# A third third-level Strassen product in half products of u (token groups 2 and 3), with three operand sums made by accumulating DMAs

## Chip, cores and metric

The kernel runs on one core of one Trainium2 chip. The metric is the device time of one execution in microseconds; the kernel before takes 812.7 us (median of three runs, 812.04 to 813.1). All data are float32.

## What is computed

The reference takes x of shape (4, 1024, 1024), four sequences of 1024 tokens. It normalises each token, and then

```python
g    = sigmoid(einsum('btd,ed->bte', u, gate_w) + gate_b)    # u is the normalised x
u_g  = u * g                                                 # its mean over a sequence enters d_eff
...                                                          # a recurrence over u_g gives s
h    = silu(xr @ w1.T)                                       # xr: the 4096 normalised tokens
h    = silu(h @ w3.T)
h    = h @ w2.T
for k in range(TOP_K):                                       # two of eight experts for each token
    out = out.at[indices_k[:, k]].add(gates[:, k:k + 1] * h) # only rows 0 to 7 are ever written
x    = x + s * silu(out)
```

Only the first eight rows of `out` differ from zero, so only those need the recurrence. What costs time is three products with 1024 x 1024 weights: `gate_w` (called g), `w1` (called u) and `w3` (called m).

## The kernel before

The 4096 tokens are taken in four groups of 1024 (`sb` = 0 to 3). Group 0 computes g, u and m, groups 1 to 3 compute u and then m, so that the order of the stages is u and g of group 0, m0, u1, m1, u2, m2, u3, m3. (Rows 0 to 7 lie in the first sequence, which is group 0, so g is needed for group 0 alone.)

Each stage is a 1024 x 1024 x 1024 product. It is done as Strassen's algorithm (Winograd's form) on two levels: seven half products `i`, in the order 1, 2, 5, 6, 7, 4, 3 for u (`order`), each of 512 x 512 x 512, and in each of these seven products of 256 x 256 x 256, the *steps* 0 to 6 of `Half.step`. One such product is four matmuls of 128 x 128 weights against 256 columns (`small`). A `block` is an operand of 128 x 4 x 512 values, a `quarter` one of 128 x 512. The left operand of half product 1, 2 and 4 is a block of tokens; that of 5, 6, 3 and 7 is a sum s1, s2, s4, s3 of blocks (`S_OF`): s1 = a21 + a22, s2 = s1 - a11, s4 = a12 - s2, s3 = a11 - a21. From its operand `left_sums` makes four quarters for the second level. All of this is subtraction on POOL (four instructions of 128x512 for a block in groups 1 to 3). The sums of the weights are made in group 0 or 1, kept in HBM (`kept`) and loaded again in the later groups.

In groups 1 to 3 some of the 256-cubed products are themselves split by Strassen: seven matmuls of 128 columns in place of four of 256. Such a product is called a *leaf*. `leaves_of` gives their number in a half product: two in u of groups 2 and 3 and in m of group 3, one elsewhere. Each leaf needs four sums of its token operand (`token_thirds`: three POOL instructions, one of 128x256 and two of 128x128) and four of its weights (`weight_thirds`: four instructions of 128x128, once, in group 1 for u; then `load_thirds`). `Half.third` issues its matmuls in phases: "a", "b", "c" write into the PSUM tile W and add from it into the result `dst` on DVE; "2" puts the rest of the first leaf into Y, "3" the rest of the second into Z, and phase "0" is the addition of the first product from the PSUM tile X.

Two half products are interleaved. Each has a place on a time line in units of one product (some 1.7 us), seven units apart; `at(place, f)` queues work, `run_todo` emits it, and all instructions stay in the program order thus made on each engine. With S the start of a half product, its steps 0 to 6 stand at S + 0, 2, 4.5, 5.5, 8, 6, 10.5, its phases "0", "a", "b", "c" at S + 1.9, 5.2, 7.5, 8.8. Within one period of seven units PE therefore runs:

1. step 0 of the current half product (into X),
2. phase "b" of the previous one,
3. its step 4 (into the previous X),
4. its phase "c",
5. step 1 of the current one (Z),
6. step 6 of the previous one (its X, the last),
7. step 2 of the current one (X again, accumulating on what step 0 left),
8. phase "a", steps 3 (Y) and 5 (Z) of the current one.

Since step 2 adds into the same X bank, it has to wait until DVE has read step 0's result out of it (phase "0"). DVE takes its work in order: in this period it is, from item 3 on, the addition of step 4, of phase "c", of step 0 (phase "0"), of step 1, step 6 and step 2.

When the previous half product is 6 or 7, each finished quarter is also added to another block (`whole`); one operand of that addition is first copied into PSUM by ACT (`to_bank`: a Y tile for the first two quarters, a tile of the tag "rows" for the other two; there is one PSUM buffer for each of these tags). These additions stand in DVE's order after the addition that completes the quarter. For 7 the result is final and ACT applies SiLU to it (`done`).

SP issues all loads and stores, in order. Buffers (20 blocks, 24 quarters) are handed out in the order in which they were given back.

Of the kernel before, what the change touches and what calls it, by code (L numbers as in the profile page):

```python
# [22 lines left out]
def kernel(  # L23
# [624 lines left out]
        op_t[kind, sb, i] = t  # L648

    def load_kept_sum(kind, sb, i, j):  # L650
        o = quarter()
        sync.dma_start(o.tile, kept[{"u": "w1", "m": "w3"}[kind], i, j])
        op_ts[kind, sb, i, j] = o

# [137 lines left out]

    BANKS = {("u", 0): (0, 1), ("m", 0): (0,)}

    def s1(kind, sb, n):
        while (kind, sb, (1, 0)) not in left:
            yield 0.25
        a22 = left[kind, sb, (1, 1)]
        o = block(1 + n)
        if (kind, sb) in BANKS:  # L800
            a21 = left[kind, sb, (1, 0)]
            yield from with_bank(o, a21, a22, (3, 0, 1, 2), op=ALU.add, of=BANKS[kind, sb])
        else:
            a21 = left[kind, sb, (1, 0)]
            for q in (3, 2, 0, 1):
                pool.tensor_tensor(o[:, q], a21[:, q], a22[:, q], ALU.add)
                yield 0.25
        a21.drop()
        a22.drop()
        left[kind, sb, "s1"] = o  # L810

    def s2(kind, sb, n):
        while (kind, sb, "s1") not in left:
            yield 0.25
        p, a11 = left[kind, sb, "s1"], left[kind, sb, (0, 0)]
        o = block(2 * n)
        if sb == 0:
            yield from with_bank(o, p, a11, (2, 3, 0, 1), of=BANKS[kind, sb])
        else:
            for q in (3, 2, 0, 1):  # L820
                pool.tensor_tensor(o[:, q], p[:, q], a11[:, q], ALU.subtract)
                yield 0.25
        p.drop()
        a11.drop()
        left[kind, sb, "s2"] = o

    def s4(kind, sb, n):

        while (kind, sb, "s2") not in left:
            yield 0.25  # L830
        o, a12 = left[kind, sb, "s2"], left[kind, sb, (0, 1)]
        if (kind, sb) == ("m", 0):
            yield from with_bank(o, o, a12, (2, 3, 0, 1), True, of=(0, 2))
        else:
            for q in (2, 3, 0, 1):
                (pool if sb else dve).tensor_tensor(o[:, q], a12[:, q], o[:, q], ALU.subtract)
                yield 0.5
        a12.drop()
        left[kind, sb, "s4"] = o

    def s3(kind, sb, n):
        a11, a21 = left[kind, sb, (0, 0)], left[kind, sb, (1, 0)]
        o = block(n)
        if (kind, sb) == ("m", 0):
            yield from with_bank(o, a11, a21, (2, 3, 0, 1), of=(0, 2))
        else:
            for q in (2, 3, 0, 1):
                (pool if sb else dve).tensor_tensor(o[:, q], a11[:, q], a21[:, q], ALU.subtract)
                yield 0.5
        a11.drop()  # L850
        a21.drop()
        left[kind, sb, "s3"] = o
# [28 lines left out]
    def is_third(kind, sb, i):  # L881
        return sb > 0 and kind != "g"

    BOTH = (("u", 2), ("u", 3), ("m", 3))

    def leaves_of(kind, sb):
        return 2 if (kind, sb) in BOTH else 1

    def cut(t):
        return t.rearrange("p (k n) -> p k n", n=P)  # L890

    def token_thirds(kind, sb, i, leaf):

        if leaf:
            a = cut(left_q[kind, sb, i, 3].tile)
        else:
            a = cut(left[kind, sb, S_OF[i]][:, 1])
        t = quarter()
        o = cut(t.tile)
        third_s[kind, sb, i, leaf] = t  # L900
        pool.tensor_tensor(
            o[:, 0:2], a[:, 1:2].to_broadcast([P, 2, P]), a[:, 0::3], ALU.subtract
        )
        yield 1
        pool.tensor_tensor(o[:, 2], a[:, 0], o[:, 1], ALU.subtract)
        pool.tensor_tensor(o[:, 3], a[:, 2], o[:, 2], ALU.subtract)

    def weight_thirds(kind, sb, i, leaf):

        name = {"u": "w1", "m": "w3"}[kind]  # L910
        op = op_t[kind, sb, i]
        t = quarter() if leaf else None
        o = t.tile if leaf else op[:, 1]
        b, c = cut(op[:, 2 + leaf]), cut(o)
        p = b
        eng = pool
        if leaf and kind == "u":
            eng = dve
            b = cut(ps_acc.tile([P, H], F32, tag="rows", name=f"raw_{i}"))
            act.copy(b.rearrange("p k n -> p (k n)"), p.rearrange("p k n -> p (k n)"))  # L920
            yield 0.6
        eng.tensor_tensor(c[:, 1], b[:, 1], p[:, 0], ALU.subtract)
        eng.tensor_tensor(c[:, 2], b[:, 3], c[:, 1], ALU.add)
        if eng is pool:
            yield 1
        eng.tensor_tensor(c[:, 3], b[:, 2], c[:, 2], ALU.subtract)
        eng.tensor_tensor(c[:, 0], b[:, 1], p[:, 3], ALU.add)
        yield 1.5
        d = dramp.tile([P, 2 * Q], F32, tag=f"{name}_{i}_t{leaf}", name=f"{name}_{i}_t{leaf}")
        sync.dma_start(d, o)  # L930
        kept[name, i, "t", leaf] = d
        if leaf:
            t.drop()

    def load_thirds(kind, sb, i, leaf):
        kept_sum = kept[{"u": "w1", "m": "w3"}[kind], i, "t", leaf]
        if leaf:
            o = quarter()
            third_t[kind, sb, i] = o
            sync.dma_start(o.tile, kept_sum)  # L940
        else:
            sync.dma_start(op_t[kind, sb, i][:, 1], kept_sum)
# [17 lines left out]
    class Half:  # L960
# [37 lines left out]
        def third(self, phase):  # L998
# [4 lines left out]
                self.first(0, self.X)  # L1003
                return
            sides = [(cut(self.A[:, 1]), cut(self.t[:, 2]), cut(self.t[:, 1]))]
            if n == 2:
                a = left_q[key + (3,)].tile if phase in "a3" else self.A[:, 1]
                sides.append((cut(a), cut(self.t[:, 3]), cut(third_t[key].tile)))
            sides = [p + (cut(third_s[key + (l,)].tile),) for l, p in enumerate(sides)]

            c12, c21 = (1, 2) if self.rows_first else (2, 1)
# [17 lines left out]
            if phase == "a":  # L1029
                self.W = ps_w.tile([P, 2 * Q], F32, tag="W", name=f"W_{self.tag}")  # L1030
                w = cut(self.W)
                for l, (a, b, T, S) in enumerate(sides):
                    go(w[:, l], a[:, 0], b[:, 0], l == 0)
                for l, (a, b, T, S) in enumerate(sides):
                    go(w[:, 2 + l], S[:, 1], T[:, 1])
                add(0, w[:, 0:n], False)
                add(slice(c12, 4, 3 - c12), w[:, 2 : 2 + n], True)
            elif phase == "b":
                w = cut(self.W)
                for l, (a, b, T, S) in enumerate(sides):  # L1040
# [2 lines left out]
            elif phase == "c":  # L1043
# [1 line left out]
                for l, (a, b, T, S) in enumerate(sides):  # L1045
                    go(w[:, l], S[:, 0], T[:, 0], False, l == n - 1)
                add(slice(c21, 4, 3 - c21), w[:, 0:n], True)
                for l in range(n):
                    third_s[key + (l,)].drop()
                if n == 2:  # L1050
                    third_t[key].drop()
                if self.i == 6 and self.rows_first:
                    at(self.place + 9, self.whole, 0)
                else:
                    self.whole(0)
                if n == 2 and self.i in (6, 7):
                    at(self.place + 9.1, self.whole, 1)
                elif n == 2:
                    self.whole(1)
            elif phase == "2":  # L1060
                self.Y = ps_y.tile([P, 2 * Q], F32, tag="Y", name=f"Y_{self.tag}")
# [3 lines left out]
            elif phase == "3":  # L1065
                direct(cut(self.Z), 1, False)
                dve.tensor_add(self.dst[:, 1], self.Z, self.dst[:, 1])

        def step(self, n):
            if n == 0:  # L1070
# [38 lines left out]
            elif n == 4:  # L1109
# [1 line left out]
                self.more(3, self.X)  # L1111
                s[2].drop()
                ts[2].drop()
            elif n == 5 and is_third(self.kind, self.sb, self.i) and leaves_of(self.kind, self.sb) == 2:
                self.third("3")
                s[3].drop()
            elif n == 5:
# [1 line left out]
                self.more(1, self.Z)  # L1119
                s[3].drop()  # L1120
            elif n == 6:
                go(self.X, A[:, 3], ts[3].tile, False, True)
                self.first(2, self.X)
                self.whole(2)
                ts[3].drop()
            if n == (7 if self.plain else 6):
# [64 lines left out]

    def to_bank(kind, sb, q):

        if q == 0 or q == 1 and leaves_of(kind, sb) == 2:
            ps = ps_y.tile([P, H], F32, tag="Y", name="by_Y")
        elif kind == "u":
            ps = ps_acc.tile([P, H], F32, tag="rows", name="by_rows")
# [214 lines left out]
    for kind, sb, i, plain in line:  # L1412
# [5 lines left out]
            at(S + 2 - 8, left_sums, kind, sb, i, n)  # L1418
        if is_third(kind, sb, i):
            if i in (6, 7):  # L1420
                for q, place in enumerate((7.6, 9.02 if leaves_of(kind, sb) == 2 else 5, 9.3, 7.2)):
                    at(S + place, to_bank, kind, sb, q)
            for phase, place in (("0", 1.9), ("a", 5.2), ("b", 7.5), ("c", 8.8)):
                at(S + place, h.third, phase)
            at(S - 1, token_thirds, kind, sb, i, 0)
            if leaves_of(kind, sb) == 2:
                at(S + 1.5, token_thirds, kind, sb, i, 1)
            if sb == 1:
                at(S - 3, weight_thirds, kind, sb, i, 0)
            else:  # L1430
                at(S - 9, load_thirds, kind, sb, i, 0)
            if leaves_of(kind, sb) == 2:
                at(S - 4, load_thirds, kind, sb, i, 1)
            elif (kind, sb) in (("u", 1), ("m", 2)):
                at(S + (7 if kind == "u" else 2.5), weight_thirds, kind, sb, i, 1)
        if kind != "g" and sb > 0:
            at(S - 10, load_kept, kind, sb, i)
            for j in range(4):
                at(S + (2, 4, 8, 10.5)[j] - 9, load_kept_sum, kind, sb, i, j)

    for sb in range(NS):
        n = 2 if sb == 0 else 1
        U = {i: start["u", sb, i] for i in range(1, 8)}
        at(U[5] - (13.5 if sb > 1 else 7 if sb else 9), s1, "u", sb, n)
        at(U[5] - (9 if sb > 1 else 6), s2, "u", sb, n)
        at(U[7] - 10, s3, "u", sb, n)
        at(U[3] - (8.6 if sb else 13), s4, "u", sb, n)
        if sb == 0:
            at(U[5] + 2, route, sb)
        M = {i: start["m", sb, i] for i in range(1, 8)}  # L1450
# [248 lines left out]
```

## Time and profile before

| | |
|---|---|
| median of three runs | 812.7 us (812.04 to 813.1) |
| the profiled execution | 812.3 us |
| its span, first to last instruction | 810.5 us |
| granted TensorE clock | 0.999 |
| stage u1, from | 268 us |
| stage u2, from / to | 442.7 / 532.8 us |
| stage u3, from / to | 617 / 707 us |
| queue of SP's DMAs | 200.80 MB, 68.8% of 16 engines' span |

The profile is of one execution. It lists for each engine the busy time and the number of instructions: PE is TensorE's matmul, PEld its weight load, DVE VectorE, ACT ScalarE, POOL GpSimd. A float32 matmul of the program stands in the profile as two matmul records. A busy PE is not PE at its peak; the spacing of its instructions in the timeline says what they cost. Line numbers mean little here, since a helper records every operation (line 89); the tiles' names tell what an instruction is: X_u is the X tile of a u half product, `b` a block, `q` a quarter, `by_rows` and `by_Y` the copies that `to_bank` makes. "out<-in" gives what is written and read.

### The profile page before, as it was taken

How to read it: one execution, taken by the hardware profiler on the slowest of the kernel's cores; microseconds unless marked ns; L12 is line 12 of the kernel's file. 1: busy time of each engine (PE TensorE's matmuls, PEld its weight loads, DVE VectorE, ACT ScalarE, POOL GpSimd, SP SyncE). 2: the span in 40 equal slices, each digit the busy share in tenths (PEclk: the TensorE clock that was granted, in tenths of full speed). 3: DMA queues.
4: the chain of work that ended last, by engine and by line, in shares of the span. 5: the costliest groups of instructions: out<-in, count | busy, mean ns of one | idle time of the engine just before them, and what ended most of it. 6: DMA issues, size and time to landing. Idle time of an engine off the chain costs nothing.

```text
span 810.5 us, 12848 instructions
## 1 busy us (share of the span) xinstructions
PE 802.8 (99%) x4463; PEld 700.3 (86%) x4463; DVE 539.9 (67%) x1040; ACT 276.4 (34%) x489; POOL 673.5 (83%) x719
## 2 busy tenths in 40 slices
PE   8999999999999999999999999999999999999997
PEld 7888888888888878888888788998888799999985
DVE  5986598766487746853878466745886376748664
ACT  1245116876332116742122136622232022230221
POOL 2799796956999699899993997999994997999930
PEclk9999999999999999999999999999999999999999
DMA  9946609464986759869968768739987566854820
GB/s 334 420 188 235 233 21 363 188 237 147 393 305 223 265 178 326 294 229 353 378 238 290 268 239 299 243 128 410 373 271 240 181 221 225 275 177 156 321 109 2
DMA packets 73071, 202.15 MB, mean 249 GB/s; under 512 B 8384, under 2 KB 11696, under 8 KB 66736
## 3 DMA queue, kind: packets, MB, share of 16 engines
q1 hardware_dynamic: 72688, 200.80, 68.8%
q8 instruction: 36, 0.59, 0.3%
q10 hardware_dynamic: 320, 0.54, 0.2%
q14 instruction: 27, 0.22, 0.1%
HBM read 170.84 MB, written 47.21 MB: 269 GB/s over the span
## 4 chain that ended last, share of the span: by engine, by line
PE 84%; POOL 8%; DMA 4%; issue 2%; DVE 1%; SPq 0%; ACT 0%; POOLq 0%
PE X_u L89 22%; PE X_m L89 18%; PE Z_u L89 10%; PE Z_m L89 8%; PE X_g L89 6%; POOL q L89 5%; POOL b L89 4%; PE W_u L89 4%; PE Z_g L89 3%; PE Y_u L89 3%; PE Y_m L89 3%; PE W_m L89 2%; PE acc L89 2%; PE plT L89 2%; DMA b<-in_x 1%
## 5 line engine op out<-in xcount | busy, mean ns | idle before, releaser
L89 POOL TENSOR_TENSOR q<-b 128x512 f32<-128x512 f32 (+2 forms) x210 | 233.7, 1129 | 46.1 <-DVE b L89 22.8
L89 ACT ACTIVATE b<-b 128x512 f32<-128x512 f32 (+1 forms) x152 | 103.4, 694 | 293.7 <-DVE b L89 276.4
L89 POOL TENSOR_TENSOR b<-b,b 128x512 f32<-128x512 f32 x120 | 150.8, 1277 | 48.0 <-DVE b L89 30.3
L89 POOL TENSOR_TENSOR q<-b,q 128x512 f32<-128x512 f32 (+1 forms) x196 | 171.9, 887 | 4.0
L89 PE MATMUL X_m<-q,q 128*128 128x256 f32 x448 | 106.2, 380 | 0.0
L89 PE MATMUL X_u<-q,q 128*128 128x256 f32 x432 | 102.5, 380 | 0.0
L89 PEld LDWEIGHTS X_m<-q,q 128*128 128x128 f32 x448 | 83.2, 190 | 12.1 <-POOL q L89 0.9
L89 DVE TENSOR_TENSOR b<-X_u,b 128x512 f32<-128x512 f32 x87 | 59.9, 688 | 47.0 <-PE X_u L89 46.3
L89 PEld LDWEIGHTS X_u<-q,q 128*128 128x128 f32 x432 | 79.7, 190 | 10.8 <-issue 1.3
L89 DVE TENSOR_TENSOR b<-X_m,b 128x512 f32<-128x512 f32 x88 | 60.4, 687 | 40.1 <-PE X_m L89 39.9
L89 DVE TENSOR_TENSOR b<-b,bc 128x1024 f32<-128x1024 f32 x56 | 67.9, 1212 | 8.8 <-ACT bc L89 8.7
L89 POOL TENSOR_TENSOR q<-q,b 128x512 f32<-128x512 f32 x56 | 71.5, 1277 | 0.2
L89 PE MATMUL X_u<-b,b 128*128 128x256 f32 x248 | 58.6, 380 | 0.0
L89 PE MATMUL Z_u<-q,q 128*128 128x256 f32 (+1 forms) x244 | 56.6, 368 | 0.0
L89 PE MATMUL Z_m<-q,q 128*128 128x256 f32 (+1 forms) x238 | 55.7, 373 | 0.0
L89 PE MATMUL X_m<-b,b 128*128 128x256 f32 x224 | 52.9, 379 | 0.0
L89 PE MATMUL X_m<-q,b 128*128 128x256 f32 x224 | 52.9, 379 | 0.0
L89 DVE TENSOR_TENSOR b<-W_u,b 128x256 f32<-128x256 f32 (+1 forms) x84 | 38.9, 484 | 20.7 <-PE W_u L89 20.1
L89 PEld LDWEIGHTS X_u<-b,b 128*128 128x128 f32 x248 | 46.0, 190 | 6.3 <-DVE b L89 0.6
L89 PE MATMUL X_u<-b,q 128*128 128x256 f32 x216 | 51.3, 380 | 0.0
L89 DVE TENSOR_TENSOR b<-Z_m,b 128x512 f32<-128x512 f32 x48 | 33.0, 688 | 24.6 <-PE Z_m L89 24.3
L89 PEld LDWEIGHTS Z_u<-q,q 128*128 128x128 f32 x244 | 43.6, 191 | 4.8 <-POOL q L89 0.4
(214 smaller groups left out, 1447.1 us busy)
## 6 DMA issues: line engine op xcount, KB each, us to landing
q<-w SPq DMA_DIRECT2D x168, 256.0 KB, 5.3
b<-in_w SPq DMA_DIRECT2D x18, 1024.0 KB, 10.6
b<-in_xT SPq DMA_DIRECT2D x15, 1024.0 KB, 10.7
w<-q SPq DMA_DIRECT2D x56, 256.0 KB, 6.2
b<-in_x SPq DMA_DIRECT2D x12, 1024.0 KB, 9.5
b<-w_T SPq DMA_DIRECT2D x24, 512.0 KB, 5.9
b<-in_w SPq DMA_DIRECT2D x20, 512.0 KB, 6.8
w_T<-b SPq DMA_DIRECT2D x8, 1024.0 KB, 4.1
```

The costliest lines, as they stand in the source:

```text
L89: r = f(*args, **kwargs)
```

## The change

In u of groups 2 and 3 a half product has three leaves in place of two: step 6, the last product into the X bank, becomes a leaf too (phase "4": three matmuls of 128 columns into X, one addition). Phases "a", "b" and "c" write three columns of blocks in place of two and the additions are half as wide again; the second part of phase "a" goes to a PSUM tile `z` of the tag "rows" of its own, since W is full. Before them the third quarter of `dst` must hold a value, which ACT writes (phase "i": zero, or a copy of the previous result, or nothing where it is already in place).

The sums for the third leaf are new: `token_thirds` on POOL (three instructions per half product), the weights' in group 1 on DVE from a copy that ACT makes into the tag "rows" (`weight_thirds`, at S + 10.6), seven stores, and in groups 2 and 3 fourteen loads of 256 KB. The fourth kept quarter of the weights is loaded 5.3 units sooner in groups 2 and 3.

In u of groups 1 to 3 the sums s2, s3 and s4 are no longer subtracted on POOL: ACT writes the negated operand into the new block (four instructions of 128x512), and POOL issues a DMA that adds the other operand to it. s4 gets a block of its own (before, it was made in place of s2). The three are also placed sooner.

```diff
+    def by_dma(o, seed, place):
+        for q in range(4):
+            act.activation(o[:, q], seed[:, q], AF.Copy, scale=-1.0)
+            yield 0.5
+        while place not in left:
+            yield 0.25
+        yield 3 if place[2] == "s1" else 1
+        pool.dma_start(o.tile, left[place].tile, accum_op=ALU.add)
...
     def s2(kind, sb, n):
+        a11 = left[kind, sb, (0, 0)]
+        if kind == "u" and sb > 0:
+            o = block(2 * n)
+            yield from by_dma(o, a11, (kind, sb, "s1"))
...
     def s4(kind, sb, n):
+        elif kind == "u" and sb > 0:
+            p, o = o, block()
+            yield from by_dma(o, p, (kind, sb, (0, 1)))
+            p.drop()
...
     def s3(kind, sb, n):
+        elif kind == "u" and sb > 0:
+            yield from by_dma(o, a21, (kind, sb, (0, 0)))
...
-    BOTH = (("u", 2), ("u", 3), ("m", 3))
+    LEAVES = {("u", 2): 3, ("u", 3): 3, ("m", 3): 2}
     def leaves_of(kind, sb):
-        return 2 if (kind, sb) in BOTH else 1
+        return LEAVES.get((kind, sb), 1)
...
     def token_thirds(kind, sb, i, leaf):
-        if leaf:
+        if leaf == 1:
             a = cut(left_q[kind, sb, i, 3].tile)
         else:
-            a = cut(left[kind, sb, S_OF[i]][:, 1])
+            a = cut(left[kind, sb, S_OF[i]][:, 1 + leaf])
...
     def weight_thirds(kind, sb, i, leaf):
-        b, c = cut(op[:, 2 + leaf]), cut(o)
+        held = op_ts[kind, sb, i, 3] if leaf == 2 else None
+        b, c = cut(held.tile if held else op[:, 2 + leaf]), cut(o)
...
             if phase == "a":
                 self.W = ps_w.tile([P, 2 * Q], F32, tag="W", name=f"W_{self.tag}")
                 w = cut(self.W)
+                if n < 3:
+                    z = w[:, 2 : 2 + n]
+                else:
+                    z = cut(ps_acc.tile([P, 2 * Q], F32, tag="rows", name=f"z_{self.tag}"))[:, 0:n]
                 for l, (a, b, T, S) in enumerate(sides):
                     go(w[:, l], a[:, 0], b[:, 0], l == 0)
                 for l, (a, b, T, S) in enumerate(sides):
-                    go(w[:, 2 + l], S[:, 1], T[:, 1])
+                    go(z[:, l], S[:, 1], T[:, 1], n > 2 and l == 0)
                 add(0, w[:, 0:n], False)
-                add(slice(c12, 4, 3 - c12), w[:, 2 : 2 + n], True)
+                add(slice(c12, 4, 3 - c12), z, True)
...
+            elif phase == "4":
+                direct(cut(self.X), 2, False)
+                dve.tensor_add(self.dst[:, 2], self.X, self.dst[:, 2])
+                for t in (third_s, third_t):
+                    t[key + (2,)].drop()
+            elif phase == "i":
+                if self.prev is None:
+                    act.activation(
+                        cut(self.dst[:, 2]),
+                        ones.unsqueeze(1).to_broadcast([P, 4, P]),
+                        AF.Copy,
+                        scale=0.0,
+                    )
+                elif self.prev is not self.dst:
+                    act.copy(self.dst[:, 2], self.prev[:, 2])
...
             elif n == 6:
-                go(self.X, A[:, 3], ts[3].tile, False, True)
-                self.first(2, self.X)
+                if is_third(self.kind, self.sb, self.i) and leaves_of(self.kind, self.sb) > 2:
+                    self.third("4")
+                else:
+                    go(self.X, A[:, 3], ts[3].tile, False, True)
+                    self.first(2, self.X)
                 self.whole(2)
...
+            if leaves_of(kind, sb) > 2:
+                at(S, token_thirds, kind, sb, i, 2)
+                at(S + 3.7, h.third, "i")
...
+            if leaves_of(kind, sb) > 2:
+                at(S - 3.5, load_thirds, kind, sb, i, 2)
+            if (kind, sb) == ("u", 1):
+                at(S + 10.6, weight_thirds, kind, sb, i, 2)
...
-                at(S + (2, 4, 8, 10.5)[j] - 9, load_kept_sum, kind, sb, i, j)
+                need = 5.2 if j == 3 and leaves_of(kind, sb) > 2 else (2, 4, 8, 10.5)[j]
+                at(S + need - 9, load_kept_sum, kind, sb, i, j)
...
-        at(U[5] - (9 if sb > 1 else 6), s2, "u", sb, n)
-        at(U[7] - 10, s3, "u", sb, n)
-        at(U[3] - (8.6 if sb else 13), s4, "u", sb, n)
+        at(U[5] - (12 if sb else 6), s2, "u", sb, n)
+        at(U[7] - (18 if sb else 10), s3, "u", sb, n)
+        at(U[3] - (17 if sb else 13), s4, "u", sb, n)
```

More of the change, by code (lines that the diff above doesn't have):

```diff
@@ L650, in load_kept_sum @@
     def load_kept_sum(kind, sb, i, j):
-        o = quarter()
+        o = quarter(2 if (kind, sb, j) == ("u", 1, 3) else 1)
         sync.dma_start(o.tile, kept[{"u": "w1", "m": "w3"}[kind], i, j])
@@ L812, in s2 @@
     def s2(kind, sb, n):
+        a11 = left[kind, sb, (0, 0)]
+        if kind == "u" and sb > 0:
+            o = block(2 * n)
+            yield from by_dma(o, a11, (kind, sb, "s1"))
         while (kind, sb, "s1") not in left:
             yield 0.25
-        p, a11 = left[kind, sb, "s1"], left[kind, sb, (0, 0)]
-        o = block(2 * n)
-        if sb == 0:
+        p = left[kind, sb, "s1"]
+        if kind == "m" or sb == 0:
+            o = block(2 * n)
+        if kind == "u" and sb > 0:
+            pass
+        elif sb == 0:
             yield from with_bank(o, p, a11, (2, 3, 0, 1), of=BANKS[kind, sb])
@@ L927, in weight_thirds @@
         eng.tensor_tensor(c[:, 0], b[:, 1], p[:, 3], ALU.add)
+        if held:
+            held.drop()
         yield 1.5
@@ L938, in load_thirds @@
             o = quarter()
-            third_t[kind, sb, i] = o
+            third_t[kind, sb, i, leaf] = o
             sync.dma_start(o.tile, kept_sum)
@@ L1005, in third @@
             sides = [(cut(self.A[:, 1]), cut(self.t[:, 2]), cut(self.t[:, 1]))]
-            if n == 2:
+            if n > 1:
                 a = left_q[key + (3,)].tile if phase in "a3" else self.A[:, 1]
-                sides.append((cut(a), cut(self.t[:, 3]), cut(third_t[key].tile)))
+                sides.append((cut(a), cut(self.t[:, 3]), cut(third_t[key + (1,)].tile)))
+            if n > 2:
+                b = op_ts[key + (3,)].tile
+                sides.append((cut(self.A[:, 3]), cut(b), cut(third_t[key + (2,)].tile)))
             sides = [p + (cut(third_s[key + (l,)].tile),) for l, p in enumerate(sides)]
@@ L1047, in third @@
                 add(slice(c21, 4, 3 - c21), w[:, 0:n], True)
-                for l in range(n):
+                for l in range(min(n, 2)):
                     third_s[key + (l,)].drop()
-                if n == 2:
-                    third_t[key].drop()
+                if n > 1:
+                    third_t[key + (1,)].drop()
                 if self.i == 6 and self.rows_first:
@@ L1055, in third @@
                     self.whole(0)
-                if n == 2 and self.i in (6, 7):
+                if n > 1 and self.i in (6, 7):
                     at(self.place + 9.1, self.whole, 1)
-                elif n == 2:
+                elif n > 1:
                     self.whole(1)
@@ L1113, in step @@
                 ts[2].drop()
-            elif n == 5 and is_third(self.kind, self.sb, self.i) and leaves_of(self.kind, self.sb) == 2:
+            elif n == 5 and is_third(self.kind, self.sb, self.i) and leaves_of(self.kind, self.sb) > 1:
                 self.third("3")
@@ L1192, in to_bank @@
     def to_bank(kind, sb, q):
-        if q == 0 or q == 1 and leaves_of(kind, sb) == 2:
+        if q == 0 or q == 1 and leaves_of(kind, sb) > 1:
             ps = ps_y.tile([P, H], F32, tag="Y", name="by_Y")
@@ L1420 @@
             if i in (6, 7):
-                for q, place in enumerate((7.6, 9.02 if leaves_of(kind, sb) == 2 else 5, 9.3, 7.2)):
+                for q, place in enumerate((7.6, 9.02 if leaves_of(kind, sb) > 1 else 5, 9.3, 7.2)):
                     at(S + place, to_bank, kind, sb, q)
@@ L1425 @@
             at(S - 1, token_thirds, kind, sb, i, 0)
-            if leaves_of(kind, sb) == 2:
+            if leaves_of(kind, sb) > 1:
                 at(S + 1.5, token_thirds, kind, sb, i, 1)
+            if leaves_of(kind, sb) > 2:
+                at(S, token_thirds, kind, sb, i, 2)
+                at(S + 3.7, h.third, "i")
             if sb == 1:
@@ L1431 @@
                 at(S - 9, load_thirds, kind, sb, i, 0)
-            if leaves_of(kind, sb) == 2:
+            if leaves_of(kind, sb) > 1:
                 at(S - 4, load_thirds, kind, sb, i, 1)
-            elif (kind, sb) in (("u", 1), ("m", 2)):
+            if leaves_of(kind, sb) > 2:
+                at(S - 3.5, load_thirds, kind, sb, i, 2)
+            if (kind, sb) == ("u", 1):
+                at(S + 10.6, weight_thirds, kind, sb, i, 2)
+            if (kind, sb) in (("u", 1), ("m", 2)):
                 at(S + (7 if kind == "u" else 2.5), weight_thirds, kind, sb, i, 1)
```

## The prediction

> **What bounds the kernel now.** I read the page's busy shares first, then the mean clock and DMA share by stage, then the timeline of one period, engine by engine.
>
> ```profile
> PE 802.8 (99%) x4463; PEld 700.3 (86%) x4463; DVE 539.9 (67%) x1040; ACT 276.4 (34%) x489; POOL 673.5 (83%) x719
> ...
> PEclk9999999999999999999999999999999999999999
> ```
>
> PE is busy 99% of the span and the clock is granted in full, so a faster kernel needs less PE work, and any wait put into PE's stream lengthens the time one for one. The windows of u1 and u2 (start:end, length, then busy time and count of PE, PEld, DVE, ACT, POOL, the clock, the DMA share, GB/s) say how full the others are:
>
> ```profile
> 268.00:359.00 91.00, 91.00 (x531) 78.07 (x530) 58.88 (x147) 41.88 (x78) 78.41 (x94) 1.00 0.76 267
> 442.70:532.80 90.10, 89.76 (x572) 78.13 (x571) 55.18 (x122) 38.72 (x72) 79.45 (x88) 1.00 0.71 248
> ```
>
> POOL is the second engine (88% of u2) and DVE has 35 of 90 us free. But DVE works in order, and order decides in the period of half product 7 of u2 (PE from 497.34, DVE beside it):
>
> ```profile
> 503.41 1.89 PE L89 MATMUL X_u<-b,q 128*128 128x256 f32 x8
> 505.14 1.97 PE L89 MATMUL X_u<-q,q 128*128 128x256 f32 x8
> 506.94 0.39 PE L89 MATMUL W_u<-b,b 128*128 128x128 f32 x2
> ...
> 501.44 0.69 DVE L89 TENSOR_TENSOR b<-X_u,b 128x512 f32<-128x512 f32 x1 [1.30 <-PE X_u L89]
> 502.23 0.69 DVE L89 TENSOR_TENSOR b<-b,by_rows 128x512 f32<-128x512 f32 x1
> 502.84 0.68 DVE L89 TENSOR_TENSOR b<-W_u,b 128x512 f32<-128x512 f32 x1
> 503.63 0.69 DVE L89 TENSOR_TENSOR b<-b,by_Y 128x512 f32<-128x512 f32 x1
> 504.35 0.69 DVE L89 TENSOR_TENSOR b<-X_u,b 128x512 f32<-128x512 f32 x1
> ```
>
> The five DVE lines are the additions of step 4, `whole` of a quarter, phase "c", `whole` of another, and phase "0". The last frees the X bank at 505.04; step 2 starts into it at 505.14 and takes 1.97 where others take 1.89. This half product and the next (517 us) already stand at the edge: each takes 11.83 us (497.34 to 509.17), the undisturbed 11.76. The spacing of DVE's starts gives its rules: an addition that needs the previous one's result starts 0.10 after that one's end (501.44 + 0.69 + 0.10 = 502.23), an independent one some 0.60 after its start; step 2 starts 0.10 after the bank is read.
>
> **The change part by part.** The program's order says that the change is made: PE issues 56 fewer matmuls of 256 columns and 98 more of 128.
>
> *PE.* Eight records from 503.41 to 505.14 are four program matmuls of 256 columns, 1.73 us, 0.4325 each; ten of 128 columns, 506.94 to 509.17, take 2.23, 0.223 each. A leaf saves 4 x 0.4325 - 7 x 0.223 = 0.17 us. Half products without a leaf take 12.09 us (m0), with one 11.92 (u1), with two 11.76: 0.16 again. Fourteen leaves: -2.4 us. In one period, "b" and "c" are 0.22 longer each, step 6 is 1.06 shorter (0.67), "a" 0.45 longer.
>
> The Trainium skill ("TensorE: Matmul & The Clock Gate", Back-to-back issue gap) speaks against the leaf: it measures 81 ns for a matmul of 128 columns in a stream with weight loads, where 256 columns would take 109 by its 2.4 GHz. By that estimate a leaf would cost 7 x 81 against 4 x 109 ns, 30% more than what it replaces, on rows of this kernel +0.5 us each and +7 in all. The rows above show a half price for half the columns, and I go by them.
>
> *DVE in periods 7 and 4 of u2 and u3.* Additions from W grow by a column: 256, 384 and 512 columns take 0.42, 0.555 and 0.68, so 768 take about 0.95. Relative to the period's start (before in brackets): step 4 is 0.22 late, its addition starts at 4.33 (4.10), `whole` 5.12 (4.89), "c" 5.73 (5.50), `whole` 5.73 + 0.95 + 0.10 = 6.78 (6.29), phase "0" 7.50 to 8.19 (7.01 to 7.70), step 2 8.29 (7.80). But PE is ready earlier: step 6 now ends at 7.80 + 0.44 - 1.06 = 7.2. PE waits 1.1 us. The saving of step 6 is thus not taken, because what follows it waited for DVE anyway. Then comes a new wait: phase "a" puts its second part into `z`, of the one buffer of the tag "rows", which holds the operand of the second `whole` from there until DVE has read it. In period 7 that is at about 10.81, PE ready at 10.69: 0.2 us. In period 4 ACT is late with this copy, since SiLU stands before it:
>
> ```profile
> 519.26 0.69 DVE L89 TENSOR_TENSOR b<-b,by_rows 128x512 f32<-128x512 f32 x1 [0.58 <-ACT by_rows L89]
> ```
>
> so it is read at 11.3 and `z` waits 0.7. Period 7 ends at 12.92 for 11.83, +1.09; period 4 at 13.41 for 11.84, +1.57.
>
> *POOL in the first period.* POOL sits idle until DVE's normalisation, then makes s1 (two instructions, and after two left sums two more), then the token sums of the first leaf:
>
> ```profile
> 444.77 2.50 POOL L89 TENSOR_TENSOR b<-b,b 128x512 f32<-128x512 f32 x2 [12.14 <-DVE b L89]
> 447.22 2.51 POOL L89 TENSOR_TENSOR q<-b 128x512 f32<-128x512 f32 x2
> 449.68 2.50 POOL L89 TENSOR_TENSOR b<-b,b 128x512 f32<-128x512 f32 x2
> 452.14 0.74 POOL L89 TENSOR_TENSOR q<-q 128x256 f32<-128x256 f32 x1
> ...
> 452.93 0.49 PE L89 MATMUL W_u<-q,q 128*128 128x128 f32 x2 [0.34 <-POOL q L89]
> ```
>
> The sum finished at 452.88 releases PE at once: no reserve. The third leaf's sums are queued ahead; those of its instructions that run behind s1 (two of 128x128, 0.46 each) move the 452.14 one to some 453.1, ending 453.84. PE, which is ready for it at 452.64 with "a" longer, goes on at 453.89, and the period ends at 455.67 for 454.59: +1.08.
>
> *The other periods.* 2, 5, 6, 3 take the leaf's -0.17. The reserve of period 6's step 2 was 1.8 us and shrinks with step 6 by 1.06, to 0.7. m's first period should gain 0.61, but there ACT copies step 0 out of X after three SiLUs (from 537.60, the copy at 539.26), and the longer "c" moves that to some 539.9, step 2 to 540.55 where PE is ready at 540.08: -0.09 left.
>
> A stage makes 1.08 - 4 x 0.17 + 1.09 + 1.57 - 0.09 = +2.97; u2 and u3 together +5.9.
>
> *u1.* `weight_thirds` for the third leaf puts four DVE instructions of 128x128 (0.29 each) and an ACT copy (0.58) into the turn from 7 to 4. The same X read
>
> ```profile
> 341.53 0.69 DVE L89 TENSOR_TENSOR b<-X_u,b 128x512 f32<-128x512 f32 x1
> ```
>
> releases step 2 at 342.32 within 0.1; the chain of the copy moves it by 0.6. Bounds 0 and 1.7 (1.15 + 0.58); I take 0.6, as half of DVE's work falls into its idle 0.47 us ahead.
>
> *Hidden.* POOL loses 36 instructions of 1.277 us and gains 14 of 0.731 and 28 of 0.459: -22.9 us, and nine DMA issues. Their price has no row; from 0 to the four subtractions they replace, 5.1 each, POOL's total does not grow. I take 1.3, one such instruction, and nothing on PE. An issue waits in POOL's order for ACT's seeds and for the other operand (three units, some 5 us, after s1's last instruction); behind it stand left sums, which in u2 are made 4.3 to 7.8 us ahead of use: that much cover, after which PE pays one for one. ACT's 36 seeds of 0.63 and the four zero fills lie in its 51 idle us of u2. SP's 14 more loads land 17 us before use; seven stores of 256 KB go beside u1's other traffic. The earlier blocks for s2 to s4 take buffers that loads would have had, and the loads' lead in u1 shrinks from 18 to 12 us, still above their 5 to 11.
>
> The accumulating DMA itself: 1 MB loads land 10.6 us after issue, 1 MB stores 4.1. s2's has some 11 us from issue (about 459) to use; I take 10.6, just hidden; 4.1 is the low end, 21.2 (a read more) the high one.
>
> The Trainium skill ("DMA: Bandwidth & Descriptors", Anatomy of one DMA) gives 2.0 us + bytes / 436e3 for a DMA from GpSimd, an estimate of 4.4 us for 1 MB, without naming an accumulation. By it the transfer is hidden with 6 us to spare, and the sum stays what it is.
>
> **Sum.** 812.3 (the profiled execution) + 5.9 + 0.6 = 818.8; the median is 0.4 above that execution, so 819.2, stated as 819.
>
> **Rivals.** *PE's saving comes through (faster).* If the waits are absorbed, 812.7 - 2.4 = 810.3. For it: gapless PE, DVE busy 55 of 90 us, POOL relieved. Against: DVE's chain has no idle time in periods 7 and 4 in which to take 0.5 us more. It decides if phase "0" lands by 7.2 in the period; 8% as such, 9% for any gain.
>
> *u1's DMAs saturate.* They are busy 0.76 x 91 = 69 us. The queue's 200.80 MB took 68.8% of 810.5 us, 2.8 us/MB; three accumulations at 1 to 3 MB's price are 8 to 25, the stores 5: 82 to 99 of 91 us. From 91 on, the excess goes to PE: up to +8 us, 827. For: the shorter lead. Against: loads landed over 10 us early in the tightest place of u1. 9%.
>
> *The accumulation is slow.* At 21.2 us s2 is 10 late, POOL's reserve takes 4.3 to 7.8, and PE waits 2.4 to 5.9 in each of three stages: 826 to 837. For: no row bounds it well; against: a load's 10.6 includes waiting behind other loads. 5%.
>
> **How the numbers follow.** The forecast's own case has 78%: -0.6 to +1.1 for u1's ends, plus or minus 2.0 for the four periods' waits (1.3 and 1.8, twice) being a third off, and 0.9 for one POOL instruction of 0.46 more or less in each first period: 815.7 to 823.2. The range for 8 in 10 goes on to 813.5, where half of the waits are absorbed, and 824.5, where u1 or s2 costs some us. 0.2% is 1.6 us, about what this kernel's runs can tell from none: faster 0.09, within 0.03, slower 0.88.
>
> **What would show it.** In the new trace of u2: PE idle about 1.1 us ahead of the second X product in periods 7 and 4, released by DVE; smaller idle ahead of `z`, by DVE; idle ahead of W or `z` in the first period, by POOL; and 11.59 us for periods 5 and 6. Wrong is the forecast if periods 7 and 4 are no longer than 11.8, and the rest of it if POOL waits for a DMA at s2, or PE in u1 waits for loads.

## The result and the profile after

The changed kernel takes 821.24 us (median of five runs, 821.13 to 821.65); the kernel before, run beside it, 812.24 (811.88 to 813.1). The ratio is 1.011 with a 95% interval of 1.0095 to 1.0125: slower, as forecast, by 9.0 us where 6.5 were worked out. The profiled execution took 821.1 us with a span of 819.4.

The page's first part, and the windows of u1 and u2 (start:end, length, busy time and count of PE, PEld, DVE, ACT, POOL, the clock, the DMA share, GB/s), for the changed kernel:

```profile
PE 802.3 (98%) x4547; PEld 701.0 (86%) x4547; DVE 559.5 (68%) x1068; ACT 302.4 (37%) x538; POOL 658.9 (80%) x734
```

```profile
268.10:360.80 92.70, 91.12 (x529) 77.59 (x528) 63.92 (x171) 51.57 (x96) 65.86 (x85) 1.00 0.88 297
444.60:538.00 93.40, 90.06 (x611) 79.37 (x610) 60.81 (x122) 46.62 (x87) 78.05 (x100) 1.00 0.89 299
```

PE is busy slightly less than before (802.3 for 802.8 us) in a span that is 8.9 longer: the time went into waits. PE's rows of the view of waits (what waited, for what, us in total, times, longest) had 0.7 us for work that was not at the start or the end of the kernel; now they have:

```profile
PE X_u L89 <- POOL q L89: 2.8, 3, 0.9
PE z_u L89 <- POOL q L89: 2.2, 2, 1.1
...
PE W_u L89 <- DVE b L89: 1.1, 1, 1.1
PE z_u L89 <- DVE b L89: 0.9, 2, 0.5
PE X_u L89 <- issue: 0.9, 1, 0.9
```

The first row names POOL, and is to be read with care. Here is period 7 of u2 in the timeline of the changed kernel (it starts at 500.08), PE first, then DVE:

```profile
507.04 0.39 PE L89 MATMUL X_u<-b,q 128*128 128x128 f32 x2
508.37 1.97 PE L89 MATMUL X_u<-q,q 128*128 128x256 f32 x8 [0.94 <-POOL q L89]
...
504.40 0.69 DVE L89 TENSOR_TENSOR b<-X_u,b 128x512 f32<-128x512 f32 x1 [1.17 <-PE X_u L89]
505.20 0.69 DVE L89 TENSOR_TENSOR b<-b,by_rows 128x512 f32<-128x512 f32 x1
505.80 0.95 DVE L89 TENSOR_TENSOR b<-W_u,b 128x768 f32<-128x768 f32 x1
506.86 0.69 DVE L89 TENSOR_TENSOR b<-b,by_Y 128x512 f32<-128x512 f32 x1
507.58 0.69 DVE L89 TENSOR_TENSOR b<-X_u,b 128x512 f32<-128x512 f32 x1
```

PE's second X product starts 0.10 after DVE's read of X (507.58 + 0.69 = 508.27). The left sum from POOL that it also takes had been written 14 us earlier. An instruction with several semaphores to wait for is put down to one of them; the time of each candidate's end tells which it was. The three waits of that row and the one of the "issue" row are the same wait in periods 7 and 4 of u2 and u3.

Since PE's stream tells where each half product starts (its first matmul into a new X tile), the whole difference can be read period by period. Lengths in us; all periods not listed agree within 0.03:

| period | before | after | difference | forecast |
|---|---|---|---|---|
| u1: 6 | 11.92 | 13.26 | +1.34 | 0 |
| u1: 4 | 12.06 | 12.67 | +0.61 | +0.6 |
| u1: 3 | 11.92 | 12.02 | +0.09 | 0 |
| u2, u3: 1 | 11.91, 11.92 | 13.10, 13.10 | +1.18, +1.18 | +1.08 |
| u2, u3: 2, 6, 3 each | 19.23, 11.76, 11.76 | 19.06, 11.60, 11.60 | -0.16 to -0.17 | -0.17 |
| u2, u3: 5 | 11.76 | 11.74 | -0.02 | -0.17 |
| u2, u3: 7 | 11.84, 11.81 | 12.94, 12.92 | +1.11, +1.11 | +1.09 |
| u2, u3: 4 | 11.84, 11.84 | 13.42, 13.57 | +1.58, +1.73 | +1.57 |
| m2, m3: first | 12.48, 11.98 | 12.46, 11.96 | -0.02 | -0.09 |

u1 makes +2.04, u2 +3.34, u3 +3.49: 8.87 of the 8.9 us.

### The profile page after: what moved, and what is told of

Read it like the earlier page. It is cut to its first block, busy times and chain, and to the rows that moved or that the text cites. A ratio compares the mean times of both kernels' runs of the same rounds, so it can differ in the third digit from the quotient of the medians.

```text
span 819.4 us, 13250 instructions
## 1 busy us (share of the span) xinstructions
PE 802.3 (98%) x4547; PEld 701.0 (86%) x4547; DVE 559.5 (68%) x1068; ACT 302.4 (37%) x538; POOL 658.9 (80%) x734
## 4 chain that ended last, share of the span: by engine, by line
PE 84%; POOL 4%; DMA 4%; DVE 4%; issue 2%; ACT 1%; SPq 0%; DVEq 0%; POOLq 0%; ACTq 0%
PE X_m L89 21%; PE X_u L89 17%; PE Z_m L89 10%; PE Z_u L89 8%; PE X_g L89 6%; PE W_u L89 3%; PE Y_m L89 3%; PE Z_g L89 3%; DVE b L89 3%; PE W_m L89 3%; DMA b<-in_x 3%; PE Y_u L89 3%; POOL q L89 2%; POOL b L89 2%; PE acc L89 2%
## 5 line engine op out<-in xcount | busy, mean ns | idle before, releaser
L89 POOL TENSOR_TENSOR q<-b 128x512 f32<-128x512 f32 (+2 forms) x224 | 245.6, 1117 | 56.7 <-DVE b L89 22.9
L89 ACT ACTIVATE b<-b 128x512 f32<-128x512 f32 (+1 forms) x188 | 123.0, 679 | 242.0 <-DVE b L89 224.4
L89 POOL TENSOR_TENSOR q<-b,q 128x128 f32<-128x128 f32 (+1 forms) x224 | 187.3, 847 | 6.9 <-POOL q L89 1.8
L89 POOL TENSOR_TENSOR b<-b,b 128x512 f32<-128x512 f32 x84 | 106.0, 1281 | 29.7 <-DVE b L89 27.7
L89 PE MATMUL X_u<-q,q 128*128 128x256 f32 (+1 forms) x460 | 108.1, 374 | 4.2 <-POOL q L89 2.8
L89 PEld LDWEIGHTS X_u<-q,q 128*128 128x128 f32 x460 | 83.5, 190 | 14.8 <-POOL q L89 3.3
L89 DVE TENSOR_TENSOR b<-X_u,b 128x512 f32<-128x512 f32 x91 | 62.5, 687 | 36.8 <-PE X_u L89 36.4
L89 DVE TENSOR_TENSOR b<-W_u,b 128x128 f32<-128x128 f32 (+2 forms) x70 | 38.1, 553 | 21.9 <-PE W_u L89 19.6
L89 PEld LDWEIGHTS X_m<-q,b 128*128 128x128 f32 x224 | 42.5, 190 | 5.7
## 6 DMA issues: line engine op xcount, KB each, us to landing
b<-b POOLq DMA_DIRECT2D x9, 1024.0 KB, 11.1
```

The costliest lines, as they stand in the source:

```text
L89: r = f(*args, **kwargs)
```

## The experiments

Theory A is that of the forecast: the added time is waits of PE, for DVE's additions in periods 7 and 4, for POOL's token sums in the first period and for the weight sums in u1. The rivals blame the DMAs, or say that an engine has too much work as a whole, so that no order helps. Each kernel is the changed one but for the edit shown, unless said otherwise; the kernel before was run beside each.

**The DMAs alone.** Two leaves, as before, with the sums made by DMA:

```diff
-    LEAVES = {("u", 2): 3, ("u", 3): 3, ("m", 3): 2}
+    LEAVES = {("u", 2): 2, ("u", 3): 2, ("m", 3): 2}
...
-            if (kind, sb) == ("u", 1):
-                at(S + 10.6, weight_thirds, kind, sb, i, 2)
```

> s2, s3, s4 of u by accumulating DMAs as in the change, but two leaves in u of groups 2 and 3 as before and no third weight sums in u1. Theory A (the time lies in waits of PE for the third leaf's additions, its POOL sums and its weight sums): the time of before, 812.2 us within 0.5, with no half product of u1, u2, u3 longer than before by 0.1. Rival B (the DMAs with accumulation, their issues on POOL or their traffic cost time, most of it in u1): 814 us or more, half product 6 of u1 again 1.3 us longer.

812.59 us, ratio to before 0.9998 (0.9988 to 1.0008), and no period of u1, u2 or u3 longer by more than 0.01. The nine accumulating DMAs cost PE nothing, and bring nothing.

**The third leaf alone.** s2, s3 and s4 by POOL, at the places that they had before:

```diff
-        at(U[5] - (12 if sb else 6), s2, "u", sb, n)
-        at(U[7] - (18 if sb else 10), s3, "u", sb, n)
-        at(U[3] - (17 if sb else 13), s4, "u", sb, n)
+        at(U[5] - (9 if sb > 1 else 6), s2, "u", sb, n)
+        at(U[7] - 10, s3, "u", sb, n)
+        at(U[3] - (8.6 if sb else 13), s4, "u", sb, n)
```

> The third leaf as in the change, but s2, s3 and s4 of u subtracted on POOL at the places they had before. POOL then has 12 more instructions of 1.28 us in each u stage, 15 us. Theory A with POOL as the next bound: left sums and token sums come late, and PE waits for POOL in more half products than the first: 823 to 828 us. Rival F (POOL has room, the DMAs are not needed for the leaf): 821.2 us within 0.6, the same waits as in the change.

821.43 us (1.0114; 1.0098 to 1.0129): the time of the change, and its waits (period 4 of u3 alone is 0.15 shorter). My expectation was wrong here. The window of u2 in this run:

```profile
444.60:538.00 93.40, 90.07 (x612) 79.38 (x611) 60.90 (x122) 40.55 (x75) 89.30 (x108) 1.00 0.76 265
```

POOL (the fifth engine in the row) is busy 89.3 of 93.4 us and still delays nothing but the first period. Its other sums are made several us ahead of use, and that cover is enough. So the leaf and the DMAs are independent, and the leaf alone carries the loss.

**s1 later in u2 and u3.**

```diff
-        at(U[5] - (13.5 if sb > 1 else 7 if sb else 9), s1, "u", sb, n)
+        at(U[5] - (10.5 if sb > 1 else 7 if sb else 9), s1, "u", sb, n)
```

> The change, with s1 of u2 and u3 queued three units later, so that POOL makes the token sums of the first half product before it stands and waits for DVE's normalisation. Theory A: the wait ahead of z in the first half product (1.24 us) goes, and the 0.5 that stood there before too: 13.10 becomes 11.85 us, twice, 818.7 us. Rival D (the sums are late because POOL has too much to do there, so that a move only shifts the wait): the first half product or a following one keeps 0.8 us or more, 820.5 us or more.

818.97 us (1.0077; 1.006 to 1.0094). The first period is 11.76 us, 1.34 less than with the change and 0.16 less than before, and no other period changes. In the changed kernel's timeline POOL is held by s1's wait for DVE with the token sums queued behind it:

```profile
446.68 2.50 POOL L89 TENSOR_TENSOR b<-b,b 128x512 f32<-128x512 f32 x2 [11.35 <-DVE b L89]
449.13 2.52 POOL L89 TENSOR_TENSOR q<-b 128x512 f32<-128x512 f32 x2
451.60 1.00 POOL L89 TENSOR_TENSOR q<-b,q 128x128 f32<-128x128 f32 x2
452.56 2.50 POOL L89 TENSOR_TENSOR b<-b,b 128x512 f32<-128x512 f32 x2
455.01 0.73 POOL L89 TENSOR_TENSOR q<-q 128x256 f32<-128x256 f32 x1
...
455.79 0.71 PE L89 MATMUL z_u<-q,q 128*128 128x128 f32 x4 [1.07 <-POOL q L89]
```

The third leaf's sums (451.60) push the second leaf's to 455.01, and PE starts when that ends. None of them needs what s1 waits for.

**Phase "0" ahead of both `whole` additions** in periods 7 and 4 of u2 and u3:

```diff
-                self.more(3, self.X)
+                if self.i in (6, 7) and leaves_of(self.kind, self.sb) > 2:
+                    dve.tensor_add(self.dst[:, 3], self.X, self.dst[:, 3])
+                    at(self.place + 8.95, self.whole, 3)
+                else:
+                    self.more(3, self.X)
...
-                if self.i == 6 and self.rows_first:
+                if self.i in (6, 7) and n > 2:
+                    at(self.place + 9, self.whole, 0)
+                elif self.i == 6 and self.rows_first:
```

In this order quarter 0 of the accumulator gets the next half product's first addition before `whole` reads it, so another sum is computed in these quarters.

> The change, with phase 0 (the read of X) put ahead of the two 'whole' additions in periods 7 and 4 of u2 and u3; nothing else moves. Theory A: X is free some 0.6 us before PE comes for it, period 7 falls from 12.94 to about 11.6 and period 4 from 13.42 and 13.57 to 11.6 to 12.2 (a wait for the 'rows' buffer of up to 0.6 may stay): 815 to 816.5 us for 821.2. Rival C (PE waits in these periods for the operand, or the longer DVE work as a whole is too much, whatever its order): no period shorter by over 0.3, 820 us or more.

826.15 us (1.0159; 1.0142 to 1.0176): slower by 5, where I had expected 5 less. The wait ahead of the second X product is gone in all four periods, as theory A says. But PE now waits at `z`, by the spacing of its starts 1.07 us for 0.07 in period 7, and 2.08 and 3.33 for 0.55 and 0.70 in period 4. For the most part that is because it comes some 1.2 us sooner in these periods to a bank that is read hardly sooner. In period 4 that read is also later, by 0.35 us in u2 and 1.47 in u3: `whole` of quarter 3 comes 1.47 us later there, so ACT's SiLUs and then its next copy into "rows" come later too. And the two longest waits cost more than themselves: after them PE ran slowly (below, in the last section). The mechanism was right, the way round it was not: it moved the wait to the next bank.

**The last `whole` operand in another bank,** so that `z` has "rows" for itself:

```diff
-        elif kind == "u":
+        elif kind == "u" and not (q == 2 and leaves_of(kind, sb) > 2):
             ps = ps_acc.tile([P, H], F32, tag="rows", name="by_rows")
```

> The change, with the operand of the last 'whole' addition (quarter 2) of u2 and u3 copied into the PSUM bank 'sm' in place of 'rows', so that z need not wait until DVE has read it. Theory A: the waits ahead of z in period 4 (0.55 in u2, 0.70 in u3) and 7 (0.07) go, with the 0.1 that PE loses after each; the wait ahead of the second X product (1.1) stays: 819.5 to 820 us for 821.2. Rival E (DVE is behind as a whole there, so PE meets the same wait at the next bank, Y or Z): periods 7 and 4 as before within 0.2, 821 us.

819.95 us (1.0095; 1.008 to 1.0111). Periods 7 and 4 are each longer than before by 0.93 to 0.94, for 1.11 and 1.58 to 1.73: the waits ahead of `z` are gone, the wait ahead of X stays. That is 1.8 us less than with the change, of which the time shows 1.3: in the profiled execution period 4 of u1, which the edit does not touch, took 13.17 us for 12.67, since ACT waited 0.72 us for a load of x and so came later with the copy for the second leaf's weight sums.

**Phase "c" split.** With the last edit, and in periods 7 and 4: quarter 0 of "c", its `whole`, phase "0", then the rest of "c" and `whole` of quarter 3 (ACT's copy of the operand for quarter 1 is queued 0.1 unit sooner, too):

```diff
-                add(slice(c21, 4, 3 - c21), w[:, 0:n], True)
+                if self.i in (6, 7) and n > 2:
...
+                    part_of(0, 1)
+                    at(self.place + 8.93, lambda: part_of(1, n))
```

> The change, with quarter 2's operand in 'sm', phase c's addition in periods 7 and 4 of u2 and u3 split in two (quarter 0 first, quarters 1 and 2 after phase 0) and the 'whole' addition of quarter 3 after phase 0 as well. The order now keeps the chain of quarter 0. Theory A: phase 0 ends at about 6.9 into the period, PE comes at 7.2, and z is free when PE comes: periods 7 and 4 take 11.6 to 11.8 us for 12.94 and 13.42 to 13.57: 815 to 816 us. Rival C (the third leaf makes DVE's work there too long in any order): a period of 12.3 us or more, 818 us or more.

815.03 us (1.0036; 1.0022 to 1.0049). All four periods take 11.60 us, less than before. DVE of this run, from step 4's addition in period 7, and PE beside it:

```profile
504.81 0.69 DVE L89 TENSOR_TENSOR b<-X_u,b 128x512 f32<-128x512 f32 x1 [1.17 <-PE X_u L89]
505.48 0.42 DVE L89 TENSOR_TENSOR b<-W_u,b 128x256 f32<-128x256 f32 x1
506.01 0.69 DVE L89 TENSOR_TENSOR b<-b,by_Y 128x512 f32<-128x512 f32 x1
506.73 0.69 DVE L89 TENSOR_TENSOR b<-X_u,b 128x512 f32<-128x512 f32 x1
507.34 0.68 DVE L89 TENSOR_TENSOR b<-W_u,b 128x512 f32<-128x512 f32 x1
...
507.45 0.39 PE L89 MATMUL X_u<-b,q 128*128 128x128 f32 x2
507.68 1.89 PE L89 MATMUL X_u<-q,q 128*128 128x256 f32 x8
```

DVE has one instruction more per period than in the change, and X is read by 507.42, 0.26 before PE comes. DVE's order was the limit, not its work.

**u1: the third leaf's weight sums on POOL.**

```diff
-        if leaf and kind == "u":
+        if leaf == 1 and kind == "u":
             eng = dve
```

> The change, with the third leaf's weight sums of u1 made by POOL straight from SBUF, without ACT's copy and DVE's four instructions. Theory A (in u1 ACT's copy holds up the routing instruction that DVE waits for, and DVE's four sums stand ahead of the read of W; in period 4 ahead of the read of X): u1's half product 6 falls from 13.26 to 11.9 and 4 from 12.67 to 12.1: 819.3 us. Rival B (u1 is longer because its DMAs have more to move, stores and accumulations): u1 stays within 0.3 of its 92.7 us, 821 us.

820.71 us (1.0099; 1.0082 to 1.0116). Periods 6 and 4 of u1 take 11.93 and 12.06 again, with the same DMAs: what made them longer was the weight sums. But period 7 is 0.29 longer, and that of half product 4 in m2 0.37, of which only the first came back in later runs (more on it below). What happens in period 6 stands in DVE's timeline of the changed kernel, where `oh` is an instruction of the routing:

```profile
311.27 0.22 DVE L89 TENSOR_TENSOR oh<-pl,ix 128x64 f32<-128x64 f32 x1 [4.05 <-ACT pl L89]
311.41 1.13 DVE L89 TENSOR_TENSOR q<-raw,q 128x128 f32<-128x128 f32 x4
312.46 0.68 DVE L89 COPY b<-X_u 128x512 f32<-128x512 f32 x1
313.06 0.21 DVE L89 TENSOR_TENSOR oh<-oh,pl 128x64 f32<-128x64 f32 x1
313.19 0.61 DVE L89 TENSOR_TENSOR b<-W_u,b 128x128 f32<-128x128 f32 x2
...
313.86 0.38 PE L89 MATMUL W_u<-q,b 128*128 128x128 f32 x1 [1.07 <-DVE b L89]
```

DVE has stood for 4 us on ACT. Then the four weight sums, 1.05 us until the next start, come first, and PE's W has to wait for the additions behind them. Before, `oh` ran at 310.88 and the copy of X right behind it:

```profile
310.88 0.22 DVE L89 TENSOR_TENSOR oh<-pl,ix 128x64 f32<-128x64 f32 x1 [3.53 <-ACT pl L89]
311.02 0.68 DVE L89 COPY b<-X_u 128x512 f32<-128x512 f32 x1
```

ACT's own copy for these sums made `oh` later by a further 0.5 (311.27, with the whole trace 0.13 earlier by then).

**All of it.** First the split, s1 later, and the weight sums of half products 2 and 7 on POOL; then those of 2 and 6, and the SiLU of quarter 1 of half product 3 behind ACT's copy of X in m's first period:

```diff
-        if leaf and kind == "u":
+        if leaf and kind == "u" and not (leaf == 2 and i in (2, 6)):
...
-                if n > 1 and self.i in (6, 7):
+                if n > 1 and (self.i in (6, 7) or n > 2 and self.i == 3):
                     at(self.place + 9.1, self.whole, 1)
```

> The last one, with s1 of u2 and u3 three units later, and the third leaf's weight sums of half products 2 and 7 of u1 on POOL. Theory A: the waits add up, so their removal does too: 815.4 - 2.5 - 1.7 = 811.2 us, 810.5 to 812. Rival G (one of the removals only uncovers the next wait): over 812.5 us.

> The one before with two changes: in u1 the third leaf's weight sums of half product 6 in place of 7 are on POOL, since those of 6 stand on DVE at the end of period 7 and push everything in period 4; and the SiLU of quarter 1 of half product 3 of u2 and u3 comes after ACT's copy of X in m's first period. Theory A: period 4 of u1 falls from 12.67 to 12.06, m's first period by 0.5 twice: 811.1 - 0.6 - 1.0 = 809.5 us. Rival G (each removal uncovers another wait): 810.8 or more.

The first took 811.13 us (0.9989; 0.998 to 0.9998), the second 809.64 (0.9972; 0.9962 to 0.9983): faster than the change and than the kernel before, though the first is faster than the latter by hardly more than the noise. In the first, period 4 of u1 kept its +0.61; in the second it took 12.00, so the sums that stand in its way are those of half product 6, made at the end of period 7. m's first periods lost 0.54 each, as expected. Of u1, u2, u3 and m only two periods remain longer than before, both in u1: 7 by 0.20 and 3 by 0.09. The 0.09 belongs to the sums of half product 7, for it was absent in the first of these two runs, which had them on POOL.

Where the 0.20 comes from stands in the second run's trace, in which period 7 starts at 322.37. First ACT, then DVE:

```profile
321.65 1.06 ACT L89 ACTIVATE b<-b 128x1024 f32<-128x1024 f32 x1 [1.24 <-DMA b<-in_x]
...
322.71 2.08 ACT L89 ACTIVATE b<-b 128x512 f32<-128x512 f32 x3
...
324.79 0.58 ACT L89 COPY raw<-b 128x512 f32<-128x512 f32 x1
...
325.39 0.29 DVE L89 TENSOR_TENSOR q<-raw,b 128x128 f32<-128x128 f32 x1 [0.59 <-ACT raw L89]
```

ACT waits for a load of x, then makes three of the negated copies for the accumulating DMAs, and only then the copy from which DVE makes the second leaf's weight sums. DVE waits 0.59 us for it, and what follows on DVE is late for PE. DVE's wait was 0.76 in the first of the two runs and 0.68 in the run with all of the third leaf's weight sums on POOL.

**The same without the DMAs, and s1 later in the kernel before:**

> The same without the DMAs: s2, s3 and s4 of u subtracted on POOL as before. If POOL has room for them, as the third leaf alone showed (all periods of u2 and u3 as in the change within 0.02, but one), the time is that of the run with the DMAs within 0.5: 809.5 us. If the DMAs are needed once the other waits are gone, PE waits for POOL in u2 or u3 and it is 811 or more.

> The kernel before with s1 of u2 and u3 three units later and nothing of the change. Theory A: PE's wait of 0.5 us ahead of the second leaf's sum in the first half product of u2 and u3 goes, twice: 811.2 us, 1.0 less than before. Else the wait moves and it stays at 812.2.

Without the DMAs 810.12 us (0.9975; 0.9966 to 0.9984), 0.5 above the run with them. The interval overlaps that run's; the one period that differs much is 3 of u3, longer by 0.84 for a wait on DVE's read of X. There one small DVE instruction of the recurrence took 1.17 us where it took 0.17 with the DMAs:

```profile
696.07 1.17 DVE L89 TENSOR_SCALAR um<-um 128x8 f32<-128x8 f32 x1
```

It ended 0.03 us after a subtraction on POOL (695.95 to 697.21). Whether POOL held it up, and whether it does so in every execution, was not tried. Period 7 of u1 is as before here: ACT makes no negated copies and does not wait for that load, and DVE finds its operand ready. It is as before in the change as well, where period 6 is longer and ACT's copy in time, and in the run with the DMAs and two leaves, so its 0.20 needs the DMAs together with the moved weight sums. The kernel before with s1 later took 811.41 us (0.999; 0.9982 to 0.9999), each first period 0.6 shorter. So of the 2.8 us that the best kernel gains, some 1.1 have nothing to do with the change. Against this kernel, period by period, the best one is 2.1 us shorter from u2 to m3 and 0.2 longer in u1.

## Why the prediction was right, and where it fell short

- **Periods 7 and 4.** Forecast +1.09 and +1.57, measured +1.11 and +1.58 (1.73 in u3). The walk through DVE's order held start by start: phase "0" was put at 7.50 into period 7 and ran at 507.58 - 500.08 = 7.50. Both waits are separate, as worked out: another bank removes that ahead of `z` alone, and the split of "c", added to it, that ahead of X.
- **The first period.** Forecast +1.08, measured +1.18, and s1 later takes it away with what stood there before.
- **The leaf.** Periods 2, 6 and 3 gained 0.16 to 0.17, and 7 and 4 reached the same 11.60 us once they did not wait. Period 5 gained only 0.02: the read of X is just late there as well, by 0.15 with the pause that follows; I had looked at the reserve of period 6 and took it for that of 5.
- **The matmul's price.** By the estimate from the Trainium skill ("TensorE: Matmul & The Clock Gate", Back-to-back issue gap) each leaf would have cost 0.5 us more. The undisturbed period with three leaves takes 11.60 for 11.76 us, so the row's half price for half the columns is right for these float32 matmuls.
- **The DMAs.** Taken as hidden; they are, with 0.9998 for the DMAs alone (the 0.20 of period 7 of u1 comes only with the weight sums moved as well). The row of the nine issues on the page of the changed kernel:

```profile
b<-b POOLq DMA_DIRECT2D x9, 1024.0 KB, 11.1
```

11.1 us to landing, where I took 10.6 from the loads. The 4.4 us estimated from the Trainium skill ("DMA: Bandwidth & Descriptors", Anatomy of one DMA) are far below it; the nearest row was the better guide. An issue takes POOL 0.92 us, where I took 1.3.
- **The step that was mis-sized is u1's,** "I take 0.6, as half of DVE's work falls into its idle 0.47 us ahead", with bounds of 0 and 1.7: it measured 2.04. The 0.6 for the turn from 7 to 4 was right (0.61). What was missing is period 6 with 1.34 and, small, period 3 with 0.09. The sums are made once for every half product, seven times; I looked at the one turn that was known to be tight, and did not go to the other places where they would stand. The trace of before showed it: DVE waited 3.5 us there for ACT, so whatever is put behind that wait comes out in a rush, with PE's banks behind it. This term makes 1.4 of the 2.4 us that the sum fell short of the periods' 8.87; the other 0.9 are small errors in u2 and u3 (6.83 for 5.9), nearly all of them on the same side: the first periods, period 5, period 4 of u3 and m's first.
- **The rivals.** The saving alone (810.3 us) did not come through, because it lay in step 6, ahead of a wait. With the waits taken out, 2.1 of its 2.4 us do; that the best kernel takes 809.64 is owed to s1's place as well. u1's DMA share rose from 0.76 to 0.88, but its periods 6 and 4 are as before once the weight sums are moved, with the same DMAs. Only the 0.2 to 0.4 us that period 7 then loses hang in part on a load that came late. The slow accumulation did not occur.

## What to carry to other kernels

Where an engine is gapless, a saving ahead of its next wait is worth nothing; ask when the bank or buffer that comes next will be free, and whether the work just added stands in the way of that. An instruction added to an in-order engine must be walked through every place in which it stands, those behind a long wait first, since an engine that is idle for a third of the stage can have no time at the point that counts. And a tightly packed order is mended by splitting the instruction that stands in front of the late one, rather than by moving it past: the moved work had its own waiter.

## What the runs showed of the hardware

A wait of some 2 us cost twice. In the run with phase "0" first, PE waited 2.08 us for DVE in period 4 of u2, until 524.90; then came windows of that run with these rows (the clock is the third figure from the end):

```profile
524.00:526.00 2.00, 1.10 (x9) 1.10 (x10) 1.74 (x3) 1.23 (x4) 2.00 (x3) 0.97 1.68 656
526.00:530.00 4.00, 4.00 (x18) 3.65 (x18) 2.22 (x4) 2.42 (x3) 2.47 (x6) 0.59 0.49 169
530.00:534.00 4.00, 4.00 (x26) 3.69 (x25) 1.69 (x4) 0.29 (x1) 0.97 (x1) 1.00 0.87 282
...
525.90:529.30 3.40, 3.40 (x15) 3.13 (x14) 2.32 (x4) 2.52 (x3) 2.57 (x6) 0.50 0.51 211
```

From 1.0 us after the wait, for 3.4 us, PE was granted half of its clock (the 0.59 is a mean over a window that reaches beyond), and its 128-column matmuls came every 0.42 us in place of 0.22. Half of 3.4 us, some 1.7, is lost to it; 0.64 of that lies in the period after, which is longer by so much than in the change (0.80 in u3, after a wait of 3.33). The waits of 1.1 us in the change had no such sequel: the clock of its u2 is 1.00. The Trainium skill ("TensorE: Matmul & The Clock Gate", What's actually happening) puts the slowing after an idle window of about 3.4 us; here a wait of 2.1 us was enough.
